# Two graph layers on one core: self-loops written into the adjacency, a shorter x1 product, and its transposition moved from TensorE to DMA

## The chip, the cores and the metric

One Trainium2 chip, one of its cores. The time is device time of one execution in microseconds; it is given as the median of several runs and for one execution that the hardware profiler recorded. The engines are called PE (TensorE, with PEld for its weight loads), DVE (VectorE), ACT (ScalarE), POOL (GpSimd) and SP (SyncE). POOL and SP issue the DMAs of this kernel.

## What is computed

The inputs are x (4096 x 64, fp32), adj (4096 x 4096, entries 0 or 1, about 16 ones in a row), and a weight and a bias for each of two layers. Cut to what matters:

```python
# layer 0
support = x @ W0
mask = (adj != 0)
rank = cumsum(mask, axis=1)
deg = rank[:, -1:]
k = minimum(deg, 100)
pos = rank - (deg - k)
w = mask * where(pos > 0, 0.5 ** (k - pos), 0)
x1 = layernorm(x + w @ support + b0)
# layer 1, W1 = [Wx; Wn]
deg = max(sum(adj, axis=1) + 1, 1)
h = (adj @ x1 + x1) / deg
out = relu(concat([x1, h], axis=1) @ W1 + b1)
out = out / max(norm(out), 1e-12)
result = layernorm(x1 + out)
```

Layer 0 weighs each neighbour by a power of two that depends on how many neighbours follow it in the row. Layer 1 needs x1 of all rows, and reads adj a second time. Multiplied by deg, the argument of layer 1's relu is deg * (x1 @ Wx + b1) + (adj @ x1 + x1) @ Wn; the normalization afterwards takes the factor out again, and the kernel works with that multiplied form.

## The kernel before, in words

adj arrives transposed and is cut into 8 slabs g of 512 output rows by 8 blocks k of 512 neighbours, so there are 64 tiles of 128 x 4 x 512. POOL loads each tile and turns it to bf16 on the way (L103); there are 32 buffers for them. The loop over the 64 steps (L539 to L578) goes through the slabs in order and within a slab through the blocks from 7 down to 0. A step does the following for its tile:

- `count` (L247, PE) counts the ones of quads of neighbours for the tiles of the next group (a chunk: 1, 2 or 4 tiles, chosen per slab at L85); at the end of a group DVE adds the counts up (`cs`, L257) and `spread` (L265 PE, L267 ACT) turns them into the base for the next group's ranks.
- `weigh` (L277, L286, PE) computes the ranks as exponents, which ACT (L293) and DVE (L294) each turn for half the tile into the bits of bf16 powers of two.
- `some_sums` (L313, PE) does up to four products of layer 1's sum adj @ x1 on tiles that are already loaded and whose x1 is ready; a tile's buffer is free for a new load once this sum has read it.
- `gather` (L304, PE) adds the previous step's weighted product to layer 0's sum.

POOL issues the load of the tile six steps ahead in every step, so a load waits when no buffer is free, and everything behind it in POOL's queue waits too.

A finished slab g goes through layer 0's end during the steps of the next slab. The table of hooks (L489 to L516) says which function is run in which step; with i = 8(g + 1): `first_pz` in step i + 1 (PE, sum times W0), `first_y`, `first_mv`, `first_s`, `first_r`, `first_x1` in steps i + 1 to i + 4 (layernorm, DVE and ACT), `first_hi`, `first_xl`, `first_lo` in steps i + 5 and i + 6. The last three split x1 in two fp16 parts side by side in `x1hl` (hi: L445 ACT, difference: L449 DVE, low times 2048: L452 ACT). From `x1hl` comes what a row needs of itself:

- `first_px` (L457, PE, step i + 6) transposes the slab's four 128 x 128 blocks into one PSUM bank.
- `first_x1T` (L460, ACT, step i + 7) copies them to the SBUF tile `x1T`.
- `first_pu` (L468 and L471, PE, step i + 7) multiplies x1T by [Wx, Wn], with W1 in three bf16 parts: twelve products of 128 columns, and one that adds b1.
- `first_c1` (L477, L478, DVE, step i + 8) forms c1 = deg * (x1 @ Wx + b1) + x1 @ Wn.

`prepare`, `prepare_w1` and `prepare_b1` (POOL) scale and split the weights once. PSUM banks of tag "m" (two of them) are shared by the counts, the spreads, pz, px and pu.

After the 64 steps comes a last stage, an order written out by hand (L756 to L924): slab 7's layer 0 end, the sums that are left (`own`, `own_half`), and for every slab `last_hT`, `last_pz` (sum times Wn), `last_z` (plus c1), relu, norm, layernorm and the store by SP. On each engine the instructions run in the order in which the program names them.

Of the kernel before, what the change touches and what calls it, by code (L numbers as in the profile page):

```python
# [9 lines left out]
F32 = mybir.dt.float32  # L10
BF16 = mybir.dt.bfloat16
FP16 = mybir.dt.float16
# [3 lines left out]
ALU = mybir.AluOpType  # L16
AX = mybir.AxisListType
PE = mybir.EngineType.PE
ACT = mybir.EngineType.Activation
DVE = mybir.EngineType.DVE  # L20
POOL = mybir.EngineType.Pool
SP = mybir.EngineType.SP

P = 128
R = 512
TB = R // P
# [3 lines left out]
STEP = 128.0  # L30
W_EXP = 127 - MAX_NEIGH
LO = 2048.0
LN_EPS = 1e-5
L2_EPS = 1e-12
QUOTA = 4
# [3 lines left out]
def adj_resnorm_kernel(  # L39
# [23 lines left out]
    nc = tc.nc  # L63
    D = x.shape[2]
    NG, NK = adjT.shape[0], adjT.shape[1]
    NB = NK * KB
    NS = NG * NK

    PSUM = bass.MemoryType.PSUM
    const = ctx.enter_context(tc.tile_pool(name="const", bufs=1))  # L70
# [11 lines left out]

    chunks = []
    for g in range(NG):
        sizes = [1] * 8 if g < 2 else [2] * 4 if g < 5 else [4] * 2  # L85
        k = NK
        for n in sizes:
            chunks.append([(g, k - 1 - i) for i in range(n)])
            k -= n
# [3 lines left out]
    A = [[None] * NK for _ in range(NG)]  # L93
# [15 lines left out]
    x1hl = const.tile([P, NB, 2 * D], FP16, name="x1hl")  # L109
    c1 = const.tile([P, NB, D], F32, name="c1")  # L110
# [34 lines left out]
    ones = const.tile([P, 1], BF16, name="ones")  # L145
# [3 lines left out]
    eps_ln = const.tile([P, 1], F32, name="eps_ln")  # L149
    nc.vector.memset(eps_ln, LN_EPS)  # L150
    ident = const.tile([P, P], F32, name="ident")
# [27 lines left out]
    nc.vector.memset(less, -STEP * MAX_NEIGH)  # L179


    wts = const.tile([P, 6 * D], F32, name="wts")
    w0_sb, wn_sb, w1_b1, b0_sb = wts[:, 0:D], wts[:, D : 2 * D], wts[:, 2 * D : 5 * D], wts[:, 5 * D : 6 * D]

    w1_parts = const.tile([P, 3, 3 * D], BF16, name="w1_parts")

    b1_parts = const.tile([P, TB, D], BF16, name="b1_parts")
    nc.vector.memset(b1_parts, 0.0)
    part = {}
    deg = const.tile([P, NB], F32, name="deg")  # L190
    least = const.tile([P, NB], F32, name="least")
    power = const.tile([P, 2 * TB], F32, name="power")
    nc.vector.memset(power, -0.5)
    x1T = const.tile([P, R], FP16, name="x1T")
    ident16 = const.tile([P, P], FP16, name="ident16")
    nc.vector.tensor_copy(ident16, ident)

    def load_weights():

# [12 lines left out]
    def split_x_low(k):  # L212
        nc.vector.tensor_scalar(xhl[:, ts(k, KB), D : 2 * D], xrs[k], LO, None, ALU.mult)

    def prepare():
        nc.gpsimd.tensor_scalar(w0_sb[0:D, :], w0_sb[0:D, :], 2.0**W_EXP, None, ALU.mult)
        nc.gpsimd.tensor_scalar(w0_sb[D:P, :], w0_sb[D:P, :], 2.0**W_EXP / LO, None, ALU.mult)

    def prepare_w1(j):
        if j == 0:  # L220
            low = wts[D:P, D : 4 * D]
            nc.gpsimd.tensor_scalar(low, low, 1.0 / LO, None, ALU.mult)
        nc.gpsimd.tensor_copy(w1_parts[:, j, :], w1_b1)
        if j < 2:
            nc.gpsimd.tensor_tensor(w1_b1, w1_b1, w1_parts[:, j, :], ALU.subtract)

    def prepare_b1():
        for j in range(3):
            row = slice(j * 32, j * 32 + 1)
            nc.gpsimd.tensor_copy(  # L230
                b1_parts[row], w1_parts[row, j, 2 * D : 3 * D].unsqueeze(1).to_broadcast([1, TB, D])
            )

    def add_b0(g):

# [76 lines left out]
    def second(acc, g, b, first, last):  # L312
        nc.tensor.matmul(acc, lhsT=x1hl[:, b, :], rhs=A[g][b // KB][:, b % KB, :], start=first, stop=last)  # L313
# [38 lines left out]
    ep = {}  # L352
# [17 lines left out]
    def root_p(v, eps, name, tag):  # L370

        n = v.shape[1]
        r = small.tile([P, n], F32, tag=tag, name=f"{tag}_{name}")
        if eps:
            nc.gpsimd.tensor_scalar(r, v, eps, None, ALU.add)
            v = r
        nc.gpsimd.tensor_tensor(r, v, power[:, 0:n], ALU.pow)  # L377
        return r
# [15 lines left out]
    def psum(n, m, name, dt=F32):  # L394

        if not banks:
            return ps_m.tile([P, n, m], dt, tag="m", name=name)
        bank = banks.pop(0)
        bank_of[name] = bank
        view = bank if dt == F32 else bank.bitcast(dt)  # L400
        return view[:, 0 : n * m].rearrange("p (n m) -> p n m", m=m)
# [7 lines left out]
    def first_pz(g):  # L409

        pz = ep["pz", g] = psum(TB, D + 1, f"pz0_{g}")
        for t in range(TB):
            nc.tensor.matmul(pz[:, t, 0:D], lhsT=ep["hT", g][:, ts(t, P)], rhs=w0_sb, start=True, stop=True)  # L413
        for t in range(TB):
            nc.tensor.matmul(pz[:, t, D : D + 1], lhsT=cs[g][:, ts(t, P)], rhs=ones, start=True, stop=True)

    def first_y(g):
        pz = ep["pz", g]
        y = ep["y", g] = epi.tile([P, TB, D], F32, tag="y", name=f"y0_{g}")
        nc.vector.tensor_tensor(y, pz[:, :, 0:D], x1[:, ts(g, TB), :], ALU.add)  # L420
        nc.vector.tensor_scalar(deg[:, ts(g, TB)], pz[:, :, D], 1.0, 1.0, ALU.add, ALU.max)

    def first_mv(g):
        ep["mv", g] = moments(ep["y", g], f"l0_{g}")
# [12 lines left out]
    def first_x1(g):  # L437
        mv, y, r = ep["mv", g], ep["y", g], ep["r", g]
        for t in range(TB):
            nc.vector.tensor_scalar(  # L440
                x1[:, g * TB + t, :], y[:, t, :], mv[:, t, 0:1], r[:, t : t + 1], ALU.subtract, ALU.mult
            )
# [8 lines left out]
    def first_lo(g):  # L451
        nc.scalar.mul(x1hl[:, ts(g, TB), D : 2 * D], ep["xl", g], LO)  # L452

    def first_px(g):
        px = ep["px", g] = psum(1, R, f"px_{g}", FP16)[:, 0, :]
        for t in range(TB):
            nc.tensor.transpose(px[:, ts(t, P)], x1hl[:, g * TB + t, :], ident16)  # L457

    def first_x1T(g):
        nc.scalar.copy(x1T, ep["px", g])  # L460

    def first_pu(g):

        pu = ep["pu", g] = psum(TB, 2 * D, f"pu_{g}")

        for t in range(TB):
            for j in range(3):
                nc.tensor.matmul(  # L468
                    pu[:, t, :], lhsT=x1T[:, ts(t, P)], rhs=w1_parts[:, j, 0 : 2 * D], start=(t, j) == (0, 0), stop=False
                )  # L470
        nc.tensor.matmul(pu[:, :, 0:D], lhsT=ones.to_broadcast([P, P]), rhs=b1_parts, start=False, stop=True)  # L471

    def first_c1(g):

        pu = ep["pu", g]
        t1 = epi.tile([P, TB, D], F32, tag="sq", name=f"t1_{g}")
        nc.vector.tensor_tensor(t1, pu[:, :, 0:D], deg[:, ts(g, TB)].unsqueeze(2).to_broadcast([P, TB, D]), ALU.mult)  # L477
        nc.vector.tensor_tensor(c1[:, ts(g, TB), :], pu[:, :, D : 2 * D], t1, ALU.add)  # L478

    hooks = defaultdict(list)  # L480

    def at(i, engine, fn, *args):
        hooks[i, engine].append((fn, args))
# [5 lines left out]
    for k in range(NK):  # L489
        i = when[0, k]  # L490
# [1 line left out]
        at(i, DVE, split_x_low, k)  # L492
    at(1, DVE, load_weights)
    at(NK - 2, POOL, prepare)
    for j in range(3):
        at(NK + 1 + j, POOL, prepare_w1, j)
    at(NK + 4, POOL, prepare_b1)
    for g in range(NG):
        at(NK * g + 3, POOL, load_x, g)
        at(NK * g + 7, POOL, add_b0, g)  # L500
    for g in range(NG - 1):
        i = NK * (g + 1)
        at(i + 1, PE, first_pz, g)
        at(i + 1, DVE, first_y, g)
        at(i + 2, DVE, first_mv, g)
        at(i + 3, "ACT, late", first_s, g)
        at(i + 3, DVE, first_r, g)
        at(i + 4, DVE, first_x1, g)
        at(i + 5, ACT, first_hi, g)
        at(i + 5, DVE, first_xl, g)  # L510
        at(i + 6, ACT, first_lo, g)
        at(i + 6, PE, first_px, g)
        at(i + 7, ACT, first_x1T, g)
        at(i + 7, PE, first_pu, g)
        at(i + 6, DVE, first_least, g)
        at(i + 8, DVE, first_c1, g)  # L516

# [19 lines left out]
    for c, chunk in enumerate(chunks):  # L539
# [4 lines left out]
        for (g, k), share in zip(chunk, shares):  # L544
            i = when[g, k]
# [6 lines left out]
            w = weigh(g, k, nr) if i == 0 else None  # L552
            for s in share:
                count(*s, s == ahead[0], s == ahead[-1])
            w = w or weigh(g, k, nr)
# [26 lines left out]
    L = NG - 1  # L582
# [10 lines left out]
    def free(name):  # L593
        banks.append(bank_of.pop(name))

    def own(g, k):

        if g not in acc:
            acc[g] = banks.pop(0)
        for b in range(k * KB, (k + 1) * KB):  # L600
            count_of[g] += 1
            second(acc[g], g, b, count_of[g] == 1, count_of[g] == len(left[g]) * KB)
# [119 lines left out]
    def last_r(u):  # L722
# [4 lines left out]
        else:  # L727
            ep["r1", name] = root_p(v, LN_EPS, name, "r1")

# [30 lines left out]
    banks.append(ps_a.tile([P, R], F32, tag="acc0", name="va0"))  # L760
    first_pz(L)
    own(5, 6)
    first_y(L)
    first_mv(L)
    own(4, 6)
# [3 lines left out]
    first_least(L)  # L769
    first_r(L)  # L770
    own(1, 6)
    first_x1(L)
    own(2, 5)
    first_hi(L)
# [1 line left out]
    first_xl(L)  # L776
    own(6, 6)
    first_lo(L)
    own(6, 7)
    own(4, 7)  # L780
    last_hT(6)
# [29 lines left out]
    last_relu(u01)  # L811
    offset(u6)
    last_sq(u01)
    first_px(L)
    last_rn(u45)
    own(3, 7)
    last_hT(2)
    first_x1T(L)
    free(f"px_{L}")
    last_ss(u01)  # L820
    u2 = unit(2)
    last_pz(u2)
# [141 lines left out]
```

## Time and profile before

| | |
|---|---|
| median of 3 runs | 247.53 us (246.74 to 248.79) |
| profiled execution | 247.51 us, of which the span of instructions 245.6 us |
| PE busy | 211.2 us, 86% of the span |
| DVE busy | 175.0 us, 71% |
| ACT busy | 134.5 us, 55% |
| POOL busy | 82.0 us, 33% (issuing loads counted) |
| share of the loads' queue in all 16 DMA engines' time | 73.8% |

In the lines of the profile, a row of a group names the line, the engine, the operation and the tiles (out<-in), then how often and how long. The page's busy digits cut the span into 40 slices of 6.14 us each; a digit is the busy share of a slice in tenths. A row of the waits names who waited for whom, the sum in us, how often and the longest. A row of the timeline begins with the start and the length in us and ends with the idle time ahead of it and what ended that. The chain of waits goes back from the last instruction to what released each; its rows begin with start and length too. Matmuls are pipelined, so the lengths of single matmuls in the timeline overlap, while the lengths in the chain don't.

### The profile page before, as it was taken

The page shows a single profiled execution, that of the slowest core. Times are in us where ns is not written, and L with a number is a line of the kernel's source. Part 1 is how long each engine was busy: PE and PEld are TensorE (multiplying, and loading weights), DVE is VectorE, ACT ScalarE, POOL GpSimd, SP SyncE. Part 2 cuts the span into 40 slices and gives each one's busy share as a digit, 9 for nine tenths or more (in the row PEclk, how much of TensorE's full clock was granted, in tenths as well). Part 3 has the DMA queues.
Part 4 walks back from the last instruction along what each step waited for, and adds up shares of the span by engine and source line. Part 5 has one row for each costly group of instructions (what it writes and reads, how often), then busy time and mean ns, then how long its engine had stood idle before and what let it go on. Part 6 is the DMA issues. An engine that isn't in the chain of part 4 may idle for free.

```text
span 245.6 us, 7439 instructions
## 1 busy us (share of the span) xinstructions
PE 211.2 (86%) x3162; PEld 98.6 (40%) x3206; DVE 175.0 (71%) x450; ACT 134.5 (55%) x202; POOL 82.0 (33%) x144
## 2 busy tenths in 40 slices
PE   8686678978999997999999999999999999997800
PEld 2222224323434442453344334433443464776600
DVE  5667587964797689479756974596559755789980
ACT  5376666674668646564655564555554521171790
POOL 8565488042124202121212121213120000277960
PEclk9999999999999999999999999999999999999985
DMA  5999999999999999999799999899970000000031
GB/s 89 184 231 248 246 218 213 215 225 213 214 223 213 214 223 215 213 185 201 133 172 169 190 183 192 165 192 185 192 141 3 3 0 3 0 9 14 3 107 43
DMA packets 11456, 37.37 MB, mean 152 GB/s; under 512 B 1568, under 2 KB 2720, under 8 KB 11424
## 3 DMA queue, kind: packets, MB, share of 16 engines
q0 software_dynamic: 9984, 35.66, 73.8%
q1 hardware_dynamic: 1440, 1.25, 1.5%
q8 instruction: 25, 0.41, 0.6%
q14 instruction: 7, 0.06, 0.1%
HBM read 69.40 MB, written 1.05 MB: 287 GB/s over the span
## 4 chain that ended last, share of the span: by engine, by line
PE 51%; DMA 20%; DVE 8%; POOL 8%; issue 5%; ACT 4%; ACTq 0%; POOLq 0%; DVEq 0%
DMA a<-in_adjT_dram 16%; PE acc L304 13%; PE acc_part L313 13%; PE v L277 6%; DMA c<-in_x_quads_dram 5%; PE cnt L247 4%; PE v L286 4%; ACT w L293 3%; POOL r L377 3%; PE va L313 2%; DVE w L294 2%; PE pz L413 2%; PE pu L468 2%; PE va L661 1%; PE rep L265 1%
## 5 line engine op out<-in xcount | busy, mean ns | idle before, releaser
L293 ACT ACTIVATE w<-v,less 128x1024 int16<-128x1024 f32 x64 | 71.3, 1114 | 58.0 <-PE v L286 45.9
L294 DVE TENSOR_SCALAR w<-v 128x1024 int16<-128x1024 f32 x64 | 78.3, 1223 | 24.7 <-PE v L286 23.3
L304 PE MATMUL acc<-w,xhl 128*128 128x512 bf16 x243 | 66.3, 379 | 2.3 <-issue 1.3
L103 POOL DMA_DIRECT2D a<-in_adjT_dram x64 | 35.2, 551 | 92.3 <-PE acc_part L313 43.8
L313 PE MATMUL acc_part<-a,x1hl 128*128 128x512 bf16 x129 | 36.4, 381 | 2.9 <-issue 2.2
L304 PEld LDWEIGHTS <-xhl 128*128 128x128 f16 x256 | 23.1, 98 | 35.5 <-issue 11.8
L313 PEld LDWEIGHTS <-x1hl 128*128 128x128 f16 x224 | 18.6, 98 | 30.6 <-issue 14.9
L277 PE MATMUL v<-a,tri 32*32 32x512 bf16 x1024 | 29.4, 384 | 0.8 <-ACT w L293 0.7
L247 PE MATMUL cnt<-a,pick 128*32 128x512 bf16 x256 | 21.5, 386 | 9.9 <-DMA a<-in_adjT_dram 9.4
L286 PE MATMUL v<-near,mine 32*32 32x512 bf16 x1024 | 28.1, 375 | 0.0
L257 DVE TENSOR_TENSOR cs<-cnt,cs 128x512 bf16<-128x512 f32 x26 | 17.8, 684 | 14.0 <-PE cnt L247 14.0
L267 ACT ACTIVATE near<-rep,most 128x512 bf16<-128x512 f32 x34 | 23.2, 683 | 5.3 <-PE rep L265 5.2
L277 PEld LDWEIGHTS <-tri 32*32 32x32 bf16 x1024 | 9.9, 87 | 22.5 <-issue 21.9
L377 POOL TENSOR_TENSOR rn<-ss,power 128x4 f32<-128x4 f32 (+1 forms) x5 | 6.3, 1273 | 28.2 <-DVE ss L683 28.1
L265 PE MATMUL rep<-cs,further 128*128 128x512 bf16 x34 | 12.9, 378 | 2.5 <-DVE cs L257 2.1
L247 PEld LDWEIGHTS <-pick 128*32 128x32 bf16 x256 | 5.0, 94 | 24.0 <-issue 12.1
L237 POOL TENSOR_TENSOR x<-x,wts 128x256 f32<-128x256 f32 x8 | 5.8, 728 | 24.4 <-DMA x<-in_x_dram 24.3
L745 ACT ACTIVATE u<-u,off,r 128x64 f32<-128x64 f32 x28 | 10.0, 427 | 0.3 <-POOL off L738 0.3
L286 PEld LDWEIGHTS <-mine 32*32 32x32 bf16 x1024 | 9.6, 87 | 1.2 <-issue 1.0
L661 PE MATMUL va<-wts,hT 128*128 128x64 f32 x64 | 8.0, 276 | 1.7 <-DVE hT L629 1.2
L259 DVE CAST cs<-cnt 128x512 bf16<-128x512 f32 x8 | 5.5, 689 | 5.1 <-PE cnt L247 5.1
L670 ACT ACTIVATE u<-u 128x256 f32<-128x256 f32 (+1 forms) x5 | 2.5, 502 | 11.7 <-DVE u L666 11.7
(139 smaller groups left out, 249.9 us busy)
## 6 DMA issues: line engine op xcount, KB each, us to landing
a<-in_adjT_dram POOLq DMA_DIRECT2D x64, 512.0 KB, 11.1
c<-in_x_quads_dram POOLq DMA_DIRECT2D x8, 128.0 KB, 11.4
x<-in_x_dram POOLq DMA_DIRECT2D x8, 128.0 KB, 8.5
out_dram<-u SPq DMA_DIRECT2D x8, 128.0 KB, 1.7
wts<-in_weights_dram SPq DMA_DIRECT2D x1, 192.0 KB, 6.8
touch<-in_x_quads_dram SPq DMA_DIRECT2D x1, 0.5 KB, 1.7
```

The source lines that it names most:

```text
L103: nc.gpsimd.dma_start(out=a, in_=adjT[g, k])
L247: nc.tensor.matmul(cnt[g][quarters[q], :], lhsT=pick[:, PW - 4 * k : PW - 4 * k + Q], rhs=A[g][k][:, q, :], start=first, stop=last,)
L257: nc.vector.tensor_tensor(new, cnt[g], cs[g], ALU.add)
L265: nc.tensor.matmul(pr, lhsT=further, rhs=cs[g], start=True, stop=True)
L267: nc.scalar.activation(near[g], pr, AF.Relu, bias=most, scale=-1.0)
L277: nc.tensor.matmul(v[e // 2][quarters[q], e % 2, :], lhsT=tri[quarters[e], :], rhs=A[g][k][quarters[e], q, :], start=True, stop=False,)
L286: nc.tensor.matmul(v[e // 2][quarters[q], e % 2, :], lhsT=mine[quarters[e], 4 * k + q, :], rhs=nr[quarters[e], :], start=False, stop=True,)
L293: nc.scalar.activation(w[:, 0:2, :], v[0], AF.Relu, bias=less)
L294: nc.vector.tensor_scalar(w[:, 2:4, :], v[1], -STEP * MAX_NEIGH, 0.0, ALU.add, ALU.max)
L304: nc.tensor.matmul(acc0[g], lhsT=xhl[:, b, :], rhs=w[:, q, :].bitcast(BF16), start=(k, q) == (NK - 1, 0), stop=(k, q) == (0, KB - 1),)
L313: nc.tensor.matmul(acc, lhsT=x1hl[:, b, :], rhs=A[g][b // KB][:, b % KB, :], start=first, stop=last)
L377: nc.gpsimd.tensor_tensor(r, v, power[:, 0:n], ALU.pow)
```

## The change

- The identity is added to adj's diagonal blocks in SBUF (`add_self`, POOL, step 8g + 12), after layer 0 has read the tile and before layer 1 does. The sum adj @ x1 then holds x1 itself.
- `first_pu` therefore multiplies by Wx alone, which is held in two fp16 parts scaled by 256: eight products of 64 columns a slab. b1 is added by DVE in `first_c1`.
- Slab 2 counts its first two tiles in groups of one.
- x1 is transposed by four DMAs on SP's queue, from `x1hl` to `x1T`, issued after `first_lo`; `first_px` and the ACT copy are gone. `first_pu` goes from step i + 7 to i + 8, `first_c1` from i + 8 to i + 9. For slab 6 both now fall in the last stage and are named there.
- The weights' DMA has five blocks of 64 columns in place of six.

```diff
--- before.py
+++ after.py
@@ -30,6 +30,7 @@
 STEP = 128.0
 W_EXP = 127 - MAX_NEIGH
 LO = 2048.0
+W_UP = 256.0
 LN_EPS = 1e-5
 L2_EPS = 1e-12
 QUOTA = 4
@@ -82,7 +83,7 @@
 
     chunks = []
     for g in range(NG):
-        sizes = [1] * 8 if g < 2 else [2] * 4 if g < 5 else [4] * 2
+        sizes = [1] * 8 if g < 2 else [1, 1, 2, 2, 2] if g == 2 else [2] * 4 if g < 5 else [4] * 2
         k = NK
         for n in sizes:
             chunks.append([(g, k - 1 - i) for i in range(n)])
@@ -179,21 +180,18 @@
     nc.vector.memset(less, -STEP * MAX_NEIGH)
 
 
-    wts = const.tile([P, 6 * D], F32, name="wts")
-    w0_sb, wn_sb, w1_b1, b0_sb = wts[:, 0:D], wts[:, D : 2 * D], wts[:, 2 * D : 5 * D], wts[:, 5 * D : 6 * D]
-
-    w1_parts = const.tile([P, 3, 3 * D], BF16, name="w1_parts")
-
-    b1_parts = const.tile([P, TB, D], BF16, name="b1_parts")
-    nc.vector.memset(b1_parts, 0.0)
+    wts = const.tile([P, 5 * D], F32, name="wts")
+    w0_sb, wn_sb, wx_sb, b1_sb, b0_sb = [wts[:, j * D : (j + 1) * D] for j in range(5)]
+
+    wx_parts = const.tile([P, 2, D], FP16, name="wx_parts")
     part = {}
     deg = const.tile([P, NB], F32, name="deg")
     least = const.tile([P, NB], F32, name="least")
     power = const.tile([P, 2 * TB], F32, name="power")
     nc.vector.memset(power, -0.5)
     x1T = const.tile([P, R], FP16, name="x1T")
-    ident16 = const.tile([P, P], FP16, name="ident16")
-    nc.vector.tensor_copy(ident16, ident)
+    ident_b = const.tile([P, P], BF16, name="ident_b")
+    nc.vector.tensor_copy(ident_b, ident)
 
     def load_weights():
 
@@ -216,20 +214,21 @@
         nc.gpsimd.tensor_scalar(w0_sb[0:D, :], w0_sb[0:D, :], 2.0**W_EXP, None, ALU.mult)
         nc.gpsimd.tensor_scalar(w0_sb[D:P, :], w0_sb[D:P, :], 2.0**W_EXP / LO, None, ALU.mult)
 
-    def prepare_w1(j):
-        if j == 0:
-            low = wts[D:P, D : 4 * D]
-            nc.gpsimd.tensor_scalar(low, low, 1.0 / LO, None, ALU.mult)
-        nc.gpsimd.tensor_copy(w1_parts[:, j, :], w1_b1)
-        if j < 2:
-            nc.gpsimd.tensor_tensor(w1_b1, w1_b1, w1_parts[:, j, :], ALU.subtract)
-
-    def prepare_b1():
-        for j in range(3):
-            row = slice(j * 32, j * 32 + 1)
-            nc.gpsimd.tensor_copy(
-                b1_parts[row], w1_parts[row, j, 2 * D : 3 * D].unsqueeze(1).to_broadcast([1, TB, D])
-            )
+    def prepare_wn():
+        low = wn_sb[D:P, :]
+        nc.gpsimd.tensor_scalar(low, low, 1.0 / LO, None, ALU.mult)
+
+    def prepare_wx():
+        for rows, up in ((slice(0, D), W_UP), (slice(D, P), W_UP / LO)):
+            nc.gpsimd.tensor_scalar(wx_sb[rows, :], wx_sb[rows, :], up, None, ALU.mult)
+        nc.gpsimd.tensor_copy(wx_parts[:, 0, :], wx_sb)
+        nc.gpsimd.tensor_tensor(wx_parts[:, 1, :], wx_sb, wx_parts[:, 0, :], ALU.subtract)
+
+    def add_self(g):
+
+        for q in range(TB):
+            d = A[g][g][:, q, ts(q, P)]
+            nc.gpsimd.tensor_tensor(d, d, ident_b, ALU.add)
 
     def add_b0(g):
 
@@ -451,31 +450,26 @@
     def first_lo(g):
         nc.scalar.mul(x1hl[:, ts(g, TB), D : 2 * D], ep["xl", g], LO)
 
-    def first_px(g):
-        px = ep["px", g] = psum(1, R, f"px_{g}", FP16)[:, 0, :]
+    def first_x1T(g):
         for t in range(TB):
-            nc.tensor.transpose(px[:, ts(t, P)], x1hl[:, g * TB + t, :], ident16)
-
-    def first_x1T(g):
-        nc.scalar.copy(x1T, ep["px", g])
+            nc.sync.dma_start(out=x1T[:, ts(t, P)], in_=x1hl[:, g * TB + t, :], transpose=True)
 
     def first_pu(g):
 
-        pu = ep["pu", g] = psum(TB, 2 * D, f"pu_{g}")
-
+        pu = ep["pu", g] = psum(TB, D, f"pu_{g}")
         for t in range(TB):
-            for j in range(3):
-                nc.tensor.matmul(
-                    pu[:, t, :], lhsT=x1T[:, ts(t, P)], rhs=w1_parts[:, j, 0 : 2 * D], start=(t, j) == (0, 0), stop=False
-                )
-        nc.tensor.matmul(pu[:, :, 0:D], lhsT=ones.to_broadcast([P, P]), rhs=b1_parts, start=False, stop=True)
+            for j in range(2):
+                nc.tensor.matmul(pu[:, t, :], lhsT=x1T[:, ts(t, P)], rhs=wx_parts[:, j, :], start=j == 0, stop=j == 1)
 
     def first_c1(g):
 
-        pu = ep["pu", g]
         t1 = epi.tile([P, TB, D], F32, tag="sq", name=f"t1_{g}")
-        nc.vector.tensor_tensor(t1, pu[:, :, 0:D], deg[:, ts(g, TB)].unsqueeze(2).to_broadcast([P, TB, D]), ALU.mult)
-        nc.vector.tensor_tensor(c1[:, ts(g, TB), :], pu[:, :, D : 2 * D], t1, ALU.add)
+        nc.vector.scalar_tensor_tensor(
+            t1, ep["pu", g], 1.0 / W_UP, b1_sb.unsqueeze(1).to_broadcast([P, TB, D]), ALU.mult, ALU.add
+        )
+        nc.vector.tensor_tensor(
+            c1[:, ts(g, TB), :], t1, deg[:, ts(g, TB)].unsqueeze(2).to_broadcast([P, TB, D]), ALU.mult
+        )
 
     hooks = defaultdict(list)
 
@@ -492,12 +486,12 @@
         at(i, DVE, split_x_low, k)
     at(1, DVE, load_weights)
     at(NK - 2, POOL, prepare)
-    for j in range(3):
-        at(NK + 1 + j, POOL, prepare_w1, j)
-    at(NK + 4, POOL, prepare_b1)
+    at(NK + 1, POOL, prepare_wx)
+    at(NK + 2, POOL, prepare_wn)
     for g in range(NG):
         at(NK * g + 3, POOL, load_x, g)
         at(NK * g + 7, POOL, add_b0, g)
+        at(min(NK * g + 12, NS - 2), POOL, add_self, g)
     for g in range(NG - 1):
         i = NK * (g + 1)
         at(i + 1, PE, first_pz, g)
@@ -509,11 +503,10 @@
         at(i + 5, ACT, first_hi, g)
         at(i + 5, DVE, first_xl, g)
         at(i + 6, ACT, first_lo, g)
-        at(i + 6, PE, first_px, g)
-        at(i + 7, ACT, first_x1T, g)
-        at(i + 7, PE, first_pu, g)
+        at(i + 6, PE, first_x1T, g)
+        at(i + 8, PE, first_pu, g)
         at(i + 6, DVE, first_least, g)
-        at(i + 8, DVE, first_c1, g)
+        at(i + 9, DVE, first_c1, g)
 
 
 
@@ -760,6 +753,7 @@
     banks.append(ps_a.tile([P, R], F32, tag="acc0", name="va0"))
     first_pz(L)
     own(5, 6)
+    first_pu(L - 1)
     first_y(L)
     first_mv(L)
     own(4, 6)
@@ -769,6 +763,8 @@
     first_least(L)
     first_r(L)
     own(1, 6)
+    first_c1(L - 1)
+    free(f"pu_{L - 1}")
     first_x1(L)
     own(2, 5)
     first_hi(L)
@@ -776,6 +772,7 @@
     first_xl(L)
     own(6, 6)
     first_lo(L)
+    first_x1T(L)
     own(6, 7)
     own(4, 7)
     last_hT(6)
@@ -811,12 +808,9 @@
     last_relu(u01)
     offset(u6)
     last_sq(u01)
-    first_px(L)
     last_rn(u45)
     own(3, 7)
     last_hT(2)
-    first_x1T(L)
-    free(f"px_{L}")
     last_ss(u01)
     u2 = unit(2)
     last_pz(u2)
@@ -947,7 +941,7 @@
     w0, b0, w1, b1 = [np.asarray(arrays.pop(f"L{s}")) for s in ("0_gnn_weight", "0_gnn_bias", "1_gnn_W", "1_gnn_b")]
     wx, wn = w1[:d], w1[d:]
     b0, b1 = [np.broadcast_to(b.reshape(1, d), (P, d)) for b in (b0, b1)]
-    arrays["weights"] = np.concatenate([np.tile(w, (2, 1)) for w in (w0, wn, wx, wn)] + [b1, b0], axis=1)
+    arrays["weights"] = np.concatenate([np.tile(w, (2, 1)) for w in (w0, wn, wx)] + [b1, b0], axis=1)
 
     nc = bacc.Bacc("TRN2", target_bir_lowering=False, num_devices=1)
     sent, args = {}, []
```

## The prediction, made before the result was known

> **What bounds the kernel now.** I read the page first (busy digits by slice), then the busy times by stretch, the waits, the chain of waits, the timeline around one slab's transposition, and last the DMA issues with the landing of every load.
>
> ```profile
> PE   8686678978999997999999999999999999997800
> DMA  5999999999999999999799999899970000000031
> ...
> 0.00:60.00 60.00, 46.31 (x737) 17.98 (x747) 40.81 (x91) 36.91 (x51) 33.98 (x66) 1.00 1.01 208
> 60.00:80.00 20.00, 18.45 (x346) 8.05 (x348) 16.44 (x35) 13.58 (x18) 5.35 (x10) 1.00 1.06 217
> 80.00:120.00 40.00, 37.92 (x645) 16.33 (x651) 31.89 (x69) 22.67 (x30) 6.53 (x12) 1.00 1.06 208
> 120.00:200.00 80.00, 77.61 (x1239) 34.54 (x1257) 54.61 (x115) 42.76 (x55) 15.26 (x27) 1.00 0.74 139
> 222.00:245.60 23.60, 8.98 (x74) 7.30 (x72) 16.15 (x92) 11.08 (x33) 13.31 (x22) 0.82 0.12 40
> ...
> PE cnt L247 <- DMA a<-in_adjT_dram: 9.4, 12, 1.4
> POOL a L103 <- PE acc_part L313: 43.8, 19, 4.7
> ```
>
> The columns of the middle rows are the stretch, its length, the busy time of PE, PEld, DVE, ACT and POOL, the clock, the DMA share and GB/s. The reader is to see four stages. Up to some 75 us the loads of adj set the pace: they land 2.5 us apart, PE waits for them (9.4 us in 12 waits), and tile 25, landed at 74.6 us, is the last that PE has to wait for. From there to 200 us PE is busy 95 to 97% of the time, and it is the loads that wait, for buffers that PE's sums free (43.8 us). Note the DMA share though: the 16 engines stay full to 120 us and are three quarters full to 200 us. From 200 to some 214 us PE works through the left-over sums; after that DVE, POOL and ACT finish the last slabs.
>
> So PE time removed between 75 and 200 us is worth its full length, and a wait put in front of PE there costs its full length. The steps that the change touches, for slab 1:
>
> ```profile
> 75.21 0.42 ACT L452 ACTIVATE x1hl<-xl 128x256 f16<-128x256 f32 x1
> 77.11 0.22 PE px L457 x4
> 79.81 0.67 PE pu L468 x12
> 80.32 0.27 PE L471 MATMUL pu<-b_parts,ones 128*128 128x256 bf16 x1
> 80.52 0.61 PE L247 MATMUL cnt<-a,pick 128*32 128x512 bf16 x8
> 82.74 1.03 PE L304 MATMUL acc<-w,xhl 128*128 128x512 bf16 x4
> 83.70 0.43 PE L277 MATMUL v<-a,tri 32*32 32x512 bf16 x16
> ...
> wts<-in_weights_dram SPq DMA_DIRECT2D x1, 192.0 KB, 6.8
> out_dram<-u SPq DMA_DIRECT2D x8, 128.0 KB, 1.7
> ```
>
> The input of the transposition is complete at 75.21 + 0.42 = 75.6 us. The transposition takes 0.22 us of PE's chain and the twelve products 0.67; the bias product adds about 0.11, the step from the last product's issue to the count after it. The last two rows are the only prices that this trace has for SP's queue: 192 KB took 6.8 us to land beside the loads (by its packet records, 3.5 us to the first packet and 0.6 from the last packet to the landing), 128 KB took 1.7 us on empty engines.
>
> **What the Trainium skill says.** "VectorE: DVE Perf Modes", section "The three transpose paths", gives 1309 ns for a 128x128 transposition by DMA and 390 ns by TensorE; the trace shows the second cheaper when four follow each other (0.22 us for all), and nothing of the first. "DMA: Bandwidth & Descriptors", sections "Queues, rings and completion order" and "Issuing engines are not separate DMA queues", says that all queues share 16 engines, which take turns packet by packet; the 6.8 against 1.7 us above agree. "TensorE: Matmul & The Clock Gate", section "Back-to-back issue gap", gives 134 cycles for 128 columns and about 60 for 64 or fewer; 0.67 / 12 = 56 ns agrees with the first.
>
> **The change part by part.** Each slab g is finished in steps i+1 to i+9, i = 8(g+1).
>
> *PE.* Removed are px (0.22 us) and the old pu (0.67 + 0.11). Added are eight products of 64 columns. The four one-column products L415, which load weights of the same shape, follow each other at 27 ns, so 8 x 27 = 0.22 us is the floor; at the 56 ns of today's products it is 0.45. I take 0.33. Saved: 0.22 + 0.78 - 0.33 = 0.67 us a slab. It counts for slabs 1 to 6, 6 x 0.67 = 4.0 us (3.3 to 4.7 by the two ends). Slab 0's falls in the stage that the loads bound, slab 7's after 217 us, where PE is not late.
>
> *Single groups in slab 2.* PE needs tile 17 one step later, and tile 19 too; its waits of 0.8 us there go. But tiles 21, 23 and 25 are still counted in pairs, and they landed 0.5, 0.3 and 0 us before PE used them: that is late next, and the gain is 0. One more count group costs DVE 0.7, ACT 0.7 and PE 0.2 us beneath that same wait.
>
> *Identity by POOL.* Four additions of 128x128 a slab. POOL's 128x256 addition L237 took 0.73 us, so about 0.37 each, 1.5 us in all. They stand ahead of the load of their step, and POOL sits idle there: 2.43 us before the load at 139.53 us. Their reader comes three steps later. Cost 0; without that cover the load would be up to 1.5 us later, and its tile has 3 us in hand. The preparation of the weights gets some 2 us shorter on POOL, also hidden.
>
> *ACT and DVE.* ACT loses the 0.59 us copy L460 of each slab; no one waits for ACT, worth 0. c1 stays two DVE instructions of about 0.42 us. In the last stage c1 of slab 6 (0.85 us) moves ahead of x1 of slab 7, whose low part was ready at 206.7 us, about 0.4 us before PE's sums asked for it; products of slab 6 also move there. I take +0.3 us (0 to 0.85).
>
> *Loads.* PE's gain shortens the time from the freeing of a buffer to the use of the tile loaded into it; the second tile of each late pair has only 0.5 to 0.8 us in hand. The transpositions put 128 KB a slab on the same engines: as 4 KB packets 2 an engine, at the loads' 0.32 us each 0.65 us a slab, 3.9 us if none of it were hidden. I take +0.5 us (0 to 3.9).
>
> *The new wait.* pu waits for four DMAs. PE works in order, so behind pu stand the next step's counts and weights, and behind them DVE and ACT. Call T the time from the end of L452 to the last landing. The cover is PE's work from there to the end of the gather of step i+8: for slab 1, 83.3 - 75.6 - 1.0 (px and old pu gone) = 6.6 us. Read in the same way, slabs 0 to 5 have 9.7, 6.6, 7.4, 7.8, 7.2 and 7.2 us, slab 6 (whose pu goes behind the first sums of the last stage) 8.0. T appears nowhere in this trace. From below: four issues of 0.33 us (SP's stores) and 1.7 us, 3 us. From above: if each of 128 rows is a packet of its own, 8 an engine and transposition, 32 turns at 0.34 us (the pace of the weights' packets) make 10.9, with 3.5 and 0.6 some 15 us. I take the skill's price four times in a row behind a full queue: 3.5 + 4 x 1.31 + 0.6 = 9.3 us up to slab 3, and 8.8 from slab 4, where the DMA share is 0.74 (first packet after 0.74 x 3.5 + 0.26 x 1.7 = 3.0). Stalls: 0, 2.7, 1.9, 1.5, 1.6, 1.6, 0.8, together 10.1 us.
>
> Sum against the profiled execution, 247.51 us (span 245.6 and 1.9 around it; the median of the runs is 247.53): 247.5 - 4.0 + 0.3 + 0.5 + 10.1 = 254.4 us.
>
> **The rivals.** *In time* (the other side): T stays under 6.6 us, because the four transpositions overlap and packets are large; pu never waits, and the time is 247.5 - 4.0 + 0.3 + 0.5 = 244.3 us. For it speaks that 192 KB landed in 6.8 us amid the loads, against it that these would be four chained instructions. It decides below T of about 7.8 us, where the stalls (about 3.2 us) equal the gain. *Row by row*: T = 15 us, 14.4 late; the stalls are 5.3, 8.4, 7.6, 7.2, 7.2, 7.2 and 6.4, 49.3 in all, 293.6 us. Against it: the skill's 1309 ns. *The loads take it back*: T is covered, but the loads lose the full 3.9 us: 247.7 us. For it the 0.5 us in hand, against it that the DMA share leaves a quarter free when it matters.
>
> **How the numbers follow.** Forecast 0.42, in time 0.30, loads 0.14, row by row 0.14. With T one us shorter or longer the forecast gives 248.6 to 261. The range, 243.2 to 268, takes in most of the first three and leaves out the low end of the first rival and row by row. About 1% (2.5 us) is what a measurement of this kernel can tell from no change. Faster by over 1%: 0.30 and 0.02 of the forecast, 0.32. Within: 0.14 and 0.05, 0.19. Slower: 0.35 and 0.14, 0.49.
>
> **What would show it.** In the profile after: DMAs of SP for x1T that land 8 to 9 us after L452; PE waiting for them before pu, 1 to 3 us in each of slabs 1 to 6, the longest in slab 1; pu at 0.2 to 0.45 us; no px; POOL's additions in idle time. Landings under 6.6 us and no such wait make the forecast wrong and the time about 244; landings of 12 us and more make it wrong the other way. Loads landing later than PE's counts after 120 us speak for the third rival.

## The result, and the profile after

The changed kernel takes 275.96 us (median of 4 executions, 271.26 to 278.17) against 248.01 us for the kernel before beside it. Executions with DMAs for x1T scatter more than others, for a reason that stays open (those of late_pu below lie between 244.2 and 255.5 us), and the ratios leave the slow ones out; of dma_only, two_transposes and late_pu2 only waits and landings are read from the profile, which is of a slow one. The ratio is 1.0999, 95% interval 1.087 to 1.1128, from 271.26 and 274.04 us. A second set of runs gave 1.0974 (1.0891 to 1.1058). The forecast was 254.4 us with a range up to 268; the sign was right, the size far too small. The profiled execution took 271.26 us, its span 269.5.

The page after (PE's and the DMA's busy tenths with the granted clock between them, now 6.74 us a slice), the group of pu, the issue of the transpositions, and the waits of the whole run:

```profile
PE   7777779970889529996999799899979999999700
PEclk9999999996599968999999999999997999999985
DMA  5999999999999984449679989999994000000021
...
L462 PE MATMUL pu<-wx_parts,x1T 128*128 128x64 f16 x48 | 5.1, 203 | 22.2 <-DMA x1T<-x1hl 22.2
x1T<-x1hl SPq DMA_TRANSPOSE x32, 5.9
wts<-in_weights_dram SPq DMA_DIRECT2D x1, 160.0 KB, 7.0
...
POOL a L104 <- PE acc_part L312: 60.4, 19, 12.3
PE cnt L246 <- DMA a<-in_adjT_dram: 7.1, 9, 1.2
```

PE, which before was at 9 of 10 or more in all slices but one from 61 to 221 us, shows two holes, in the 10th slice and in the 14th and 15th. They are waits of pu for the transposed x1: 22.2 us by this row. At the end of each hole and behind it the granted clock falls to between 5 and 8 of 10, and behind the second the DMA engines go down to 4: the loads stand still because PE frees no buffers. That is the coupling of the kernel before, read backwards (POOL's wait for PE's sums has grown from 43.8 to 60.4 us, its longest from 4.7 to 12.3). The median landing of one transposition, 5.9 us, hides what matters, so here is the timeline of PE in slab 1, in two pieces, and then the rows of the tile x1T in the stretches of slab 1 and of slab 7, where no loads are left:

```profile
90.27 1.03 PE L303 MATMUL acc<-w,xhl 128*128 128x512 bf16 x4
91.68 0.23 PE L462 MATMUL pu<-wx_parts,x1T 128*128 128x64 f16 x2 [0.38 <-DMA x1T<-x1hl]
93.99 0.23 PE L462 MATMUL pu<-wx_parts,x1T 128*128 128x64 f16 x2 [2.08 <-DMA x1T<-x1hl]
96.94 0.29 PE L462 MATMUL pu<-wx_parts,x1T 128*128 128x64 f16 x2 [2.71 <-DMA x1T<-x1hl]
99.89 0.29 PE L462 MATMUL pu<-wx_parts,x1T 128*128 128x64 f16 x2 [2.66 <-DMA x1T<-x1hl]
100.11 0.65 PE L276 MATMUL v<-a,tri 32*32 32x512 bf16 x16
...
105.59 0.43 PE L276 MATMUL v<-a,tri 32*32 32x512 bf16 x16
```

```profile
L455 SPq DMA_TRANSPOSE x1T<-x1hl x4: 1094/1176/1440, 84.0 to 87.7; - x4
DMA to landing us min/median/max: 7.7/9.6/12.1
...
L455 SPq DMA_TRANSPOSE x1T<-x1hl x4: 1095/1182/1187, 231.2 to 234.9; - x4
DMA to landing us min/median/max: 2.2/2.3/2.4
```

The three numbers after a count are the shortest, median and longest. SP needs 1.2 us to issue one transposition in either stretch. On empty engines each lands 2.3 us later; amid the loads of slab 1 the first takes 7.7 us and the fourth 12.1, and pu's pairs of products start 2.3, 3.0 and 3.0 us apart. From the end of `first_lo` to the last landing (the prediction's T) the slabs 0 to 7 took 16.7, 15.9, 10.1, 9.8, 9.3, 9.5, 6.9 and 6.1 us.

### The profile page after: what moved, and what is told of

Same layout as the page of the kernel before. It is cut to its first block, busy times and chain, and to the rows that moved or that the text cites. A ratio compares the mean times of both kernels' runs of the same rounds, so it can differ in the third digit from the quotient of the medians.

```text
span 269.5 us, 7392 instructions
## 1 busy us (share of the span) xinstructions
PE 214.6 (80%) x3094; PEld 94.2 (35%) x3135; DVE 175.5 (65%) x450; ACT 131.4 (49%) x195; POOL 92.9 (34%) x172
## 3 DMA queue, kind: packets, MB, share of 16 engines
q1 hardware_dynamic: 6560, 2.27, 3.9%
## 4 chain that ended last, share of the span: by engine, by line
PE 39%; DMA 29%; DVE 12%; POOL 6%; ACT 5%; issue 4%; SPq 1%; ACTq 0%; POOLq 0%; DVEq 0%
DMA x1T<-x1hl 18%; DMA a<-in_adjT_dram 12%; PE acc L303 9%; PE acc_part L312 9%; PE v L276 6%; PE cnt L246 4%; ACT w L292 4%; DVE w L293 3%; PE v L285 3%; PE pz L412 3%; POOL r L376 2%; DVE x L439 2%; DVE cs L256 1%; PE va L312 1%; PE va L654 1%
## 5 line engine op out<-in xcount | busy, mean ns | idle before, releaser
L104 POOL DMA_DIRECT2D a<-in_adjT_dram x64 | 35.3, 553 | 108.7 <-PE acc_part L312 60.4
L303 PE MATMUL acc<-w,xhl 128*128 128x512 bf16 x238 | 67.1, 388 | 2.4 <-issue 1.3
L312 PE MATMUL acc_part<-a,x1hl 128*128 128x512 bf16 x136 | 38.7, 393 | 2.2 <-issue 1.8
L256 DVE TENSOR_TENSOR cs<-cnt,cs 128x512 bf16<-128x512 f32 x27 | 18.4, 683 | 21.9 <-PE cnt L246 21.9
L266 ACT ACTIVATE near<-rep,most 128x512 bf16<-128x512 f32 x35 | 23.9, 683 | 4.9 <-PE rep L264 4.9
L462 PE MATMUL pu<-wx_parts,x1T 128*128 128x64 f16 x48 | 5.1, 203 | 22.2 <-DMA x1T<-x1hl 22.2
L276 PEld LDWEIGHTS <-tri 32*32 32x32 bf16 x1024 | 10.1, 88 | 24.2 <-issue 23.5
L264 PE MATMUL rep<-cs,further 128*128 128x512 bf16 x35 | 13.5, 386 | 2.4 <-DVE cs L256 1.5
L231 POOL TENSOR_TENSOR a<-a,ident_b 128x128 bf16<-128x128 bf16 x32 | 12.7, 430 | 2.9 <-PE v L276 2.8
L462 PEld LDWEIGHTS <-x1T 128*128 128x128 f16 x64 | 3.7, 100 | 26.1 <-DMA x1T<-x1hl 24.8
L236 POOL TENSOR_TENSOR x<-x,wts 128x256 f32<-128x256 f32 x8 | 5.8, 730 | 17.0 <-DMA x<-in_x_dram 16.9
## 6 DMA issues: line engine op xcount, KB each, us to landing
a<-in_adjT_dram POOLq DMA_DIRECT2D x64, 512.0 KB, 10.2
c<-in_x_quads_dram POOLq DMA_DIRECT2D x8, 128.0 KB, 11.5
```

The lines of the kernel that those rows point to most:

```text
L104: nc.gpsimd.dma_start(out=a, in_=adjT[g, k])
L231: nc.gpsimd.tensor_tensor(d, d, ident_b, ALU.add)
L256: nc.vector.tensor_tensor(new, cnt[g], cs[g], ALU.add)
L264: nc.tensor.matmul(pr, lhsT=further, rhs=cs[g], start=True, stop=True)
L266: nc.scalar.activation(near[g], pr, AF.Relu, bias=most, scale=-1.0)
L276: nc.tensor.matmul(v[e // 2][quarters[q], e % 2, :], lhsT=tri[quarters[e], :], rhs=A[g][k][quarters[e], q, :], start=True, stop=False,)
```

## The experiments

Three theories stood at the start. *Wait*: all is PE's wait at pu. *Traffic*: the transpositions' packets delay the loads. *Rest*: much of it is in the other edits. The edits are against the changed kernel where nothing else is said, and cut to what matters (`...`).

**TensorE's transposition back, all else as changed** (label pe_transpose).

```diff
+    def first_px(g):
+        px = ep["px", g] = psum(1, R, f"px_{g}", FP16)[:, 0, :]
+        for t in range(TB):
+            nc.tensor.transpose(px[:, ts(t, P)], x1hl[:, g * TB + t, :], ident16)
+
     def first_x1T(g):
-        for t in range(TB):
-            nc.sync.dma_start(out=x1T[:, ts(t, P)], in_=x1hl[:, g * TB + t, :], transpose=True)
+        nc.scalar.copy(x1T, ep["px", g])
...
-        at(i + 6, PE, first_x1T, g)
+        at(i + 6, PE, first_px, g)
+        at(i + 7, ACT, first_x1T, g)
```

> The changed kernel with one thing undone: TensorE transposes x1 again and ScalarE copies it; all else, pu in step i + 8 too, as changed. Wait theory (the loss is PE's wait at pu for the four transpositions, 28 us in the profile, and what follows from it): no wait at pu, 0.98 to 0.99 of the kernel before, about 244 us. Traffic theory (the transpositions' packets delay the loads of adj): also about 244 us. Rest theory (a good part of the loss is in the other edits, POOL's additions ahead of the loads above all): 250 to 260 us.

Measured: 0.9933 (0.9899 to 0.9968), 245.83 us. The other edits together are a gain; the rest theory falls. The gain is smaller than the 3 us expected; the run pe_early below tells why. (The 28 us of waits named in the expectation are 22.2 by the row above.)

**The kernel before with the DMA transposition alone** (dma_only): the same lines in `before`, pu in step i + 8, c1 in i + 9.

> The kernel before with the transposition by DMA alone, pu in step i + 8 and c1 in step i + 9; identity, Wx, b1 and slab 2 as before. Wait theory: the whole loss and the 3 us of the other edits' gain besides, 276 to 282 us, with 28 us of waits at pu. Rest theory: clearly less, 255 to 268 us.

Measured: 1.1158 (1.1106 to 1.1211), a median of 277.28 us; PE waited 19.8 us for x1T. Again the transposition by DMA carries the loss.

**The same DMAs, pu four steps later** (late_pu).

```diff
-        at(i + 8, PE, first_pu, g)
+        if g < NG - 2:
+            at(i + 12, PE, first_pu, g)
...
-        at(i + 9, DVE, first_c1, g)
+        if g < NG - 2:
+            at(i + 13, DVE, first_c1, g)
```

> The changed kernel with the same 32 transpositions, but pu of slabs 0 to 5 four steps later (i + 12), c1 in step i + 13. The transpositions ended at most 16.7 us after their input was ready, and i + 12 leaves some 17 to 18. Wait theory: the waits of slabs 0 to 5 go and with them nearly all of the loss, 243 to 247 us. Traffic theory: the same packets stand among the loads, so most of the loss stays, above 258 us.

Measured: 0.994 (0.9902 to 0.9978). Its rows of x1T, over the whole span and then for slab 2 alone, and the stretches in which the transpositions of slabs 1, 2 and 3 are under way (the columns are length, busy PE, PEld, DVE, ACT, POOL, clock, DMA share, GB/s):

```profile
L455 SPq DMA_TRANSPOSE x1T<-x1hl x32: 1094/1182/2052, 51.4 to 208.9; - x32
  PEld L462: 0.6, 1
DMA to landing us min/median/max: 2.2/6.6/12.3
...
L455 SPq DMA_TRANSPOSE x1T<-x1hl x4: 1095/1189/1901, 98.9 to 103.4; - x4
DMA to landing us min/median/max: 7.4/10.1/11.8
...
77.20:93.90 16.70, 16.50 (x271) 6.64 (x271) 12.55 (x28) 9.85 (x13) 3.73 (x8) 1.00 1.07 214
98.90:115.20 16.30, 16.30 (x246) 6.70 (x243) 12.15 (x25) 9.48 (x12) 5.32 (x11) 1.00 1.08 215
121.90:131.60 9.70, 9.70 (x145) 3.68 (x144) 5.70 (x8) 6.06 (x8) 2.16 (x5) 1.00 1.08 194
```

All 32 transpositions are there, and those of slabs 0 to 2 are as slow as ever (17.0, 16.8 and 16.3 us). But PE is busy through the stretches of slabs 1 to 3, and the only wait for x1T left is 0.6 us. So the loss was the wait; the traffic theory in its strong form falls. A gain over the kernel before is not shown: 0.994 rests on the six shortest of twenty executions, and the median of all is 248.4 us against 247.8. One detail tells why slab 2 took only 10.1 us in the changed kernel: there PE's standstill in slab 1 had stopped the loads, here it had not, and slab 2 took 16.3.

**One plain DMA in place of the four** (one_copy).

```diff
-        for t in range(TB):
-            nc.sync.dma_start(out=x1T[:, ts(t, P)], in_=x1hl[:, g * TB + t, :], transpose=True)
+        nc.sync.dma_start(out=x1T, in_=x1hl[:, ts(g, TB), :])
```

> The changed kernel with one plain DMA in place of the four transpositions: 128 rows of 1024 bytes, 8 packets an engine in place of 32; the transposition itself is left out. If the landing time is that of packets taking turns with the loads: about 7 us amid the loads (the weights' 160 KB took 7.0), a wait of less than 1 us at pu, 244 to 248 us in all. If any DMA on SP's queue lands late behind a full loads' queue, 12 us and more in slabs 0 and 1 and over 255 us in all.

Measured: 0.9939 (0.9909 to 0.997). Its rows of slab 0:

```profile
L454 SPq DMA_DIRECT2D x1T<-x1hl x1: 512/512/512, 51.1 to 51.1; - x1
DMA to landing us min/median/max: 7.3/7.3/7.3
```

From the end of `first_lo` it landed after 7.4 us in slab 0, 7.8 in slab 1 and 2.0 in slab 7. The same 128 KB in fewer packets, and in one DMA, are in time.

**Four plain DMAs** (four_copies): only `transpose=True` is taken out.

> The changed kernel with four plain DMAs of 128 rows of 256 bytes in place of the four transpositions; the transposition is left out. If the landing is a matter of packets taking turns with the loads: 32 packets an engine as with the transpositions, 12 to 16 us from the end of L451 to the last landing in slabs 0 and 1, waits of 3 to 8 us there, 255 to 268 us in all; on empty engines 3 to 4 us, as SP issues a plain DMA in 0.46 us. If it is the transposition itself: 7 to 8 us as with one copy, 244 to 248 us in all.

Measured: 1.0632 (1.0594 to 1.067), 247.7 x 1.0632 = 263 us. The rows of slab 1 and of slab 7, and the count of packets of the page, which for one copy, four copies and four transpositions differ as follows:

```profile
L455 SPq DMA_DIRECT2D x1T<-x1hl x4: 465/543/547, 82.5 to 84.3; - x4
DMA to landing us min/median/max: 7.5/10.3/12.9
...
L455 SPq DMA_DIRECT2D x1T<-x1hl x4: 464/552/557, 223.2 to 225.1; - x4
DMA to landing us min/median/max: 1.7/1.8/1.8
...
q1 hardware_dynamic: 2592, 2.26, 2.8%
q1 hardware_dynamic: 6048, 2.26, 3.7%
q1 hardware_dynamic: 6560, 2.27, 3.9%
```

Plain copies of the same rows land nearly as late amid the loads: T is 15.5 and 14.8 us in slabs 0 and 1, against 16.7 and 15.9 with transpositions, although SP issues them in half the time. So the transposition as such is at most 1.2 us of it. From one copy to four transpositions a slab there are (6560 - 2592) / 8 = 496 more packets, 31 an engine: 128 of 256 bytes and 32 of 4 bytes for each transposition, 10 turns an engine (a turn is one packet on one engine). On empty engines the picture is the other way round: T is 3.7 us with copies and 6.1 with transpositions, and there SP's issue is the term, 4 x 1.18 against 4 x 0.55 us.

These runs alone leave a rival: from one copy to four, the number of DMAs grows with the number of packets. The packet records of the changed kernel's slab 1 decide it. From 87.7 to 98.9 us the 512 packets of 256 bytes start in one stream, with 554 load packets of 4 KB among them, nearly one for one. Each DMA's 128 take 2.2 to 2.9 us, and the next DMA's begin 0.1 us later, so no time goes by between the DMAs. On empty engines, in slab 7, a DMA's 128 packets all start within 0.25 us. It is the packets, taking turns with those of the loads.

**Two of the four transpositions** (two_transposes; blocks 1 and 3 are left out, and x1T is set to zero once).

```diff
-        for t in range(TB):
+        for t in range(0, TB, 2):
```

> The changed kernel with only two of the four transpositions (blocks 0 and 2; the other two blocks are left out and read as zeros): half the packets, half of SP's issue time. If packets decide: 9 to 10 us to the last landing in slabs 0 and 1 (16.7 and 15.9 with four, 7.5 for the first one), under slab 0's cover and about 2 us over slab 1's; 3.6 us in slab 7; 245 to 250 us in all.

Measured: 1.0268 (1.0199 to 1.0338), 254 us, above the 245 to 250 expected. Its rows of slab 0:

```profile
L456 SPq DMA_TRANSPOSE x1T<-x1hl x2: 1232/1446/1659, 51.5 to 53.2; - x2
DMA to landing us min/median/max: 7.4/8.3/9.3
```

T is 11.0 and 10.4 us in slabs 0 and 1 and 3.6 in slab 7. The two more transpositions of the changed kernel are 20 turns an engine and cost (16.3 - 10.7) = 5.6 us on the mean of slabs 0 and 1: 0.28 us a turn. Against four copies, one copy gives (15.1 - 7.6) / 27 = 0.28 again. The loads' own packets of 4 KB take 0.32 us each, so amid the loads a packet of 256 bytes costs about one load packet's time.

**The changed kernel again, and PE kept busy through the waits** (after_again, filled_wait, filled_all). The second and third put needless products ahead of pu:

```diff
         pu = ep["pu", g] = psum(TB, D, f"pu_{g}")
+        for n in range({0: 86, 1: 78, 2: 22, 3: 18, 4: 18, 5: 20}.get(g, 0)):
+            nc.tensor.matmul(pu[:, :, :], lhsT=xhl[:, 0, :], rhs=xhl[:, 0:2, :], start=True, stop=True)
```

> The changed kernel once more, as the standard for the three beside it: 271 to 278 us, PE's clock granted at half for 17 to 25 us in all, after the waits in slabs 0 and 1.

> The changed kernel with 86 and 78 needless products of 256 columns (107 ns each, 9.2 and 8.3 us in all) put ahead of pu in slabs 0 and 1, into the bank that pu then overwrites: PE works through the wait in place of idling. Wait theory without the clock: the wait is as long, the time the same as the changed kernel's, 271 to 278. Clock theory (an idle PE is granted half the clock for some 10 us afterwards, and that costs about 6 us): no half clock in slabs 0 to 2, 264 to 269 us, although PE does more.

> The changed kernel with needless products ahead of pu in slabs 0 to 5 (86, 78, 22, 18, 18 and 20 of 256 columns), about as long as the waits. With slabs 0 and 1 filled alone, step 48 began 4 to 7 us earlier, but later waits brought half clock again, and the time was the same. Clock theory: no half clock before the last stage, 262 to 268 us. If the clock costs next to nothing in this kernel: 270 to 276 us.

Measured: 1.0974 (1.0891 to 1.1058) again, 1.1021 (1.0946 to 1.1095) with slabs 0 and 1 filled, 1.0948 (1.0912 to 1.0983) with all filled. The stretches around slab 1, first of the changed kernel, then with all filled:

```profile
83.00:100.00 17.00, 8.37 (x140) 3.36 (x134) 5.69 (x9) 6.47 (x9) 1.21 (x3) 0.90 1.06 211
100.00:108.00 8.00, 7.73 (x101) 3.49 (x102) 5.75 (x9) 2.73 (x3) 1.75 (x3) 0.78 0.39 67
...
83.00:100.00 17.00, 16.10 (x212) 10.73 (x210) 4.60 (x6) 5.54 (x7) 1.10 (x2) 1.00 1.07 209
100.00:108.00 8.00, 8.00 (x145) 3.60 (x113) 7.43 (x18) 3.96 (x5) 1.84 (x3) 1.00 0.58 98
```

With products in the wait the clock stays at 1.00; without, it falls to 0.90 and 0.78, and in the timeline above the step after slab 1's pu takes 105.59 - 100.11 = 5.48 us, against 3.88 in the filled kernel. So an idle PE does lose clock here, but the price is 1.0 us behind slab 0 (5.19 against 4.20), 1.6 behind slab 1 and 1.4 behind slab 5 (5.01 against 3.63), and the needless products make the steps that hold them 2.0 us longer in all. In the time the effect can't be told from none: the intervals of the three overlap. The clock theory's 262 to 268 us was wrong.

**Better versions** (pe_early, pairs, late_pu2). The first is the run pe_transpose with pu in step i + 7 and c1 in i + 8:

```diff
-        at(i + 8, PE, first_pu, g)
+        at(i + 7, PE, first_pu, g)
...
-        at(i + 9, DVE, first_c1, g)
+        at(i + 8, DVE, first_c1, g)
...
-    first_pu(L - 1)
...
-    first_c1(L - 1)
-    free(f"pu_{L - 1}")
```

> The changed kernel with TensorE's transposition as before and pu and c1 at their old places (i + 7 and i + 8). In the run with pu in i + 8, slab 5's and later slabs' second step was 0.3 to 0.9 us longer, pz waiting for c1 of the slab before (PSUM bank); if that is the reason, those steps return to 3.33 us and the time falls 1 to 2 us below that run's: 0.985 to 0.991 of the kernel before. If the loads take back what PE saves, no better than 0.993.

> The run beside it (TensorE's transposition, pu and c1 at their old places) with slab 2 counted in pairs again. The prediction held single groups in slab 2 worth nothing: same time within 0.3%. If they help PE over the loads there: 1 to 2 us slower than the run beside it.

> The changed kernel with its DMA transposition, pu of slabs 0 to 5 in step i + 12 and c1 in i + 13; and in the last stage pu of slab 6 one group of sums later and c1 of slab 6 behind x1 of slab 7 instead of ahead of it. With pu late the last stage took 50.9 us against 50.0 before, 0.5 of it PE's wait for slab 6's transposition. If these places were the reason: 50 us and 0.986 to 0.991 in all; if not, 0.994 as with pu late alone.

Measured: pe_early 0.9842 (0.9821 to 0.9863), 243.78 us, faster than both kernels. Rows of pe_transpose's and then pe_early's timeline (pu of slab 3, pz of slab 4) show why the place of pu matters:

```profile
128.08 0.40 PE L468 MATMUL pu<-wx_parts,x1T 128*128 128x64 f16 x8
132.10 1.08 PE L414 MATMUL pz<-wts,hT 128*128 128x64 f32 x8 [0.66 <-DVE t L473]
...
125.38 0.40 PE L468 MATMUL pu<-wx_parts,x1T 128*128 128x64 f16 x8
130.99 1.00 PE L414 MATMUL pz<-wts,hT 128*128 128x64 f32 x8
```

With pu in step i + 8 the next slab's pz waits for DVE's c1 to give up its PSUM bank. That step took 4.23 us in slab 5 and 3.63 in slabs 6 and 7; it is 3.33 in pe_early, as in the kernel before. These three waits are 1.5 of the 2 us between the two runs. With slab 2 in pairs (`[2] * 4`) it is 0.9863 (0.9837 to 0.989): the difference to pe_early, half a microsecond, can't be told from none. The second late pu (pu of slab 6 behind `own(0, 6)`, c1 of slab 6 behind `first_xl(L)`) gave 0.9987 (0.9957 to 1.0016), no better than the first (the medians of all executions are 248.6 and 248.4 us): those places were not the reason.

## Why the prediction was wrong

*The step that failed is "The new wait", in the size of T under a full queue.* That PE would wait at pu for these DMAs was right. The prediction took the Trainium skill's 1309 ns four times behind a full queue, 9.3 us, and set aside the other end it had worked out, rows as packets of their own, 15 us. In slabs 0 and 1 the rows were packets, and T was 16.7 and 15.9 us; its own sign of being wrong that way, landings of 12 us, came there. Its page "VectorE: DVE Perf Modes", section "The three transpose paths", gives that price without saying how busy the engines are; here four transpositions took 6.1 us alone and 16 us amid loads. What "DMA: Bandwidth & Descriptors", section "Queues, rings and completion order", says of turns by packet was the right mechanism, and the prediction quoted it, but T was added up from durations, and the term for the loads counted bytes (2 packets an engine and slab, where 40 went).

So *row by row* was right about T in the first slabs, but its 293.6 us took 15 us for every slab. From slab 2 on T was 10.1 to 6.1 us, with far fewer loads outstanding (issued and not landed): at most three of adj, against up to eight in slab 0. In late_pu, whose loads were not stopped, slab 2 took 16.3.

*The cover of slab 0 was mis-sized too.* It was read from the trace of before as 9.7 us, of which 1.7 were PE's waits for tiles 17 and 19. The same prediction had these waits go. In the changed kernel the last weights of that step's gather were loaded 57.97 - 51.06 = 6.9 us after `first_lo`.

*The stalls.* Each is the length of the step that holds pu less that of the same step in pe_transpose. Slab 0 had 9.9 us where none was forecast, slab 1 had 8.6 instead of 2.7. Slabs 2 to 5 had 2.2, 1.6, 1.6 and 1.8 against 1.9, 1.5, 1.6 and 1.6: that is near, but partly by luck, since few loads were outstanding there and T had other terms than the prediction gave it. Slab 6 had none (0.8 forecast). Together they are 25.7 us instead of 10.1, which is 15.6 of the 16.9 us between the profiled execution and the forecast.

*The sum.* Measured by the starts of the steps' first products with the triangle `tri`, and against pe_transpose, which differs in nothing but the transposition: steps 16 to 19 took 22.7 us instead of 13.2 (+9.5), steps 24 to 27 21.7 instead of 11.5 (+10.3, of which 1.6 is the clock), steps 28 to 62 109.6 instead of 103.3 (+6.2). The first 16 steps, steps 20 to 23 and the last stage gave back 1.0, 0.1 and 0.5. Together 24.4 us, the whole difference of the two spans (269.5 and 245.1).

*PE's saving was right.* In late_pu the step that lost the old pu went from 3.41 to 2.63 us (0.78), the one that lost px from 3.18 to 2.96 (0.22), and the one that got the new pu from 2.96 to 3.19: 0.23 us for eight products, the floor of 8 x 27 ns, not the 0.33 taken. So 0.77 us a slab against 0.67. The Trainium skill's "TensorE: Matmul & The Clock Gate", section "Back-to-back issue gap", gives about 60 cycles, or 25 ns, for up to 64 columns; here it is 0.23 / 8 = 29 ns, a little more.

*The edits counted at nothing were near it.* POOL's additions took 0.42 us each instead of 0.37, and no instruction waited for them:

```profile
L231 POOL TENSOR_TENSOR a<-a,ident_b x32: 414/420/615, 38.9 to 202.5; 128x128 bf16<-128x128 bf16 x32
```

Single groups in slab 2 gained nothing that can be measured, as forecast. *What the prediction left out*: that c1 one step later holds pz's bank, 0.3 to 0.9 us in each of three slabs, and the clock. The rival *in time* was wrong in its mechanism, T under 6.6 us. Its sum was put to the test by late_pu, where PE waits next to nothing at pu: 244.3 us was some 2 us too good by the ratio (247.8 x 0.994 = 246.3) and 4 by the median of all executions. The third rival, that the loads take it back, has a small share of that. Tile 28 of adj landed at 83.2 us in late_pu, against 82.1 in the kernel before and in pe_transpose and 81.8 in pe_early, which put no transpositions among the loads. Later on no share of it is shown, since PE's waits for tiles of adj between 75 and 200 us were no longer in late_pu (first row) than in pe_transpose (second); pe_early and the kernel before had none.

```profile
PE cnt L246 <- DMA a<-in_adjT_dram: 1.2, 3, 0.5
PE cnt L248 <- DMA a<-in_adjT_dram: 1.7, 2, 0.9
```

Where the rest of the 2 to 4 us went stays open.

## What to carry to other kernels

A small DMA that goes among a full stream of loads (here three or more outstanding) is priced by its packets per engine times about the loads' packet time, and a fixed part (here 7.6 - 9 x 0.28 = 5 us, from one_copy), not by its bytes or by its duration on empty engines; read the packet count first, and place its consumer that far behind or give it fewer, longer rows. When a cover is read from a trace, take out of it every wait that the same change removes. An in-order engine that stops also stops what feeds on the buffers it frees, so look for the second dip behind the first.

## What the runs showed of the hardware

- A 128x128 transposition of fp16 from SBUF to SBUF is 128 packets of 256 bytes and 32 of 4 bytes; SP takes 1.18 us to issue it (a plain DMA of the same rows 0.55), and it lands 2.2 to 2.4 us after the start of its issue on empty engines.
- In late_pu's slabs 0 to 2, with three to seven loads outstanding, T was 16.3 to 17.0 us; in its slabs 3 to 5, with one to three outstanding and two on the mean, 9.7 to 10.6, though the DMA share was 1.08 in the stretches of slab 2 and slab 3 alike. The share alone doesn't tell the delay; it went with the number of loads outstanding. The packet records show the difference: in slab 2 at most 18 of the 512 packets of 256 bytes start in any quarter of a microsecond, in slab 3 226 of them start in one, from 127.9 to 128.15 us. Why two loads leave such openings was not tried.
- Ahead of its last stage the changed kernel's PE was granted half its clock in spells of 3.4 to 10.2 us, during or after the waits at pu of slabs 0, 1 and 5, where PE idled 8.6, 7.8 and 1.4 us in all, but not with the 2.0, 1.2 and 1.1 us of slabs 2, 3 and 4. In the second profile of the same kernel (after_again) such a spell came behind slab 2, with 2.1 us, and none behind slab 5, with 0.9.
